# ScalarE in the order of the steps, e buffers in turn, and a shorter VectorE queue ahead of transposed steps

## The chip, the cores and the metric

The kernel runs on one core of a Trainium2 chip. Five engines work side by side, each through its own queue of instructions: TensorE (PE) multiplies matrices, VectorE (DVE) and ScalarE (ACT) work elementwise, GpSimd (POOL) gathers here, and SyncE (SP) starts DMAs. The metric is device time in microseconds (us), the median of several executions. A profile is one more execution, taken by the hardware profiler.

## The reference

The input is four images of 128 channels and 64 x 64 positions. Layer 0 normalizes in groups of channels, runs a deformable 3 x 3 convolution and adds its result to the image. A small convolution yields for every position and tap two offsets and a mask (a sigmoid); each tap then samples the image bilinearly at the offset place. Layer 1 treats the 4,096 positions as tokens of 128 channels: a layer norm; an attention of 16 heads of width 8, in which query, key and value are the same array (products of cosines), so that its score matrix is symmetric; layer norm; a feed-forward part of which only 8 channels' cosines enter; a second norm; and then a mixture of 8 experts, in which every token takes the weighted sum of its best two. In short, for each image:

```python
x = x + deformable_conv(group_norm(x))
t = tokens(x); u = layer_norm(t)
q = ring_of_cosines(u + rx)                      # 16 heads of 8
a = softmax(q @ q.T / sqrt(8)) @ q               # 4096 x 4096 per head
x1 = layer_norm(u + a @ w_comb.T + b_comb)
f  = relu((cos(x1[..., :8]) * cos(ry)) @ w1.T) @ w2.T
t  = t + layer_norm(x1 + f)
t  = t + top2_of_8_experts(layer_norm(t))
```

The largest part by far is the attention: 4 x 16 score matrices of 4096 x 4096 with one exponential for each element that is not had from symmetry.

## The kernel before

**Steps.** The attention is cut into runs. A run is a batch b, a group g of four heads and a chunk sc of 512 queries; it goes through key tiles t of 128 keys. A step is one (run, t): `scores` (line 1240) issues four matmuls on 32 rows each (line 1250) into two PSUM tiles `sc`, and two exps on ScalarE (line 1259), which write two tiles `e` of 128 x 1024. `context` (line 1263) multiplies each of the four heads' part of `e` with the values (line 1267) and adds into `acc`; at the end of a run VectorE copies `acc` out (line 1471 or 1473). There are 3,700 steps and 7,400 exps. The scores are issued `LAG` = 2 steps ahead of the context, so TensorE's order is: scores of step n + 2, some side matmuls, context of step n.

**Buffers.** `sc` comes from a pool of three PSUM buffers (line 254, two banks each), `e` from six buffers (line 1258, `bufs=6`). A buffer is free again once all that read it have done so.

**Weights from symmetry.** The exps of queries sc against keys sc + 1 are the transposes of those of queries sc + 1 against keys sc. For a step in the set `gives` the function `turn` (line 1131) has VectorE transpose the two `e` tiles in 32 x 32 blocks into a staging tile `st` (line 1141), which four DMAs store in `etd`; 396 of the 3,700 steps are such. A later run fetches them (line 1185) and multiplies them as side work in `from_turned` (line 1203). `st` has three buffers (NST), which the deformable convolution's `tr` tiles share.

**Side work.** All the rest runs beside the steps. `prepare` makes a batch's convolution and its queries, keys and values, for the batch after the one in attention; `finish` does the output projection, the feed-forward part and the experts of a chunk whose four groups are done. Both are generators. At each `yield need(...)` they ask for time on TensorE and VectorE, and the planner `Beside` decides when the next piece is emitted. It keeps a clock (`now`, 1.82 us a step) and a time up to which VectorE is booked (`dve`). A piece for VectorE is let in only if `dve - now` is at most the `backlog` that the main loop gives: 1.5 in the first runs (`streaming`), later 3.2, and 0.4 in the last three steps of a run. `beside.later(when, emit)` puts an emission off until the planner's clock reaches `when`; this is used for DMAs and for GpSimd. Up to two `finish` jobs are active at once (line 1117), and their tiles share a pool of eleven buffers (`f2`).

**Who orders the queues.** The main loop stands inside `tc.manual_schedule` (line 1395) for PE, DVE, SP and POOL: these run in the order in which the program emits them. ScalarE is not among them. Its order, and which of a pool's buffers an exp's tile gets, come from the framework's scheduler, which works with its own estimate of when instructions end.

**ScalarE's other instructions.** The mask's exp `mk` in `rows_and_weights` (line 559, eight times) and the router's exp `ex` in `experts` (line 1017, 32 times), and at the start some DMAs that load weights.

Of the kernel before, what the change touches and what calls it, by code (L numbers as in the profile page):

```python
# [9 lines left out]
F32 = mybir.dt.float32  # L10
I32 = mybir.dt.int32
F32R = mybir.dt.float32r
AF = mybir.ActivationFunctionType
ALU = mybir.AluOpType
AX = mybir.AxisListType
PE = mybir.EngineType.PE
DVE = mybir.EngineType.DVE
SP = mybir.EngineType.SP
POOL = mybir.EngineType.Pool
PSUM = bass.MemoryType.PSUM  # L20
DRAM = bass.MemoryType.DRAM

P = 128
# [176 lines left out]
def need(pe=0.0, dve=0.0, lat=0.0, hold=False, after=0.0):  # L200

    return pe, dve, lat, hold, after


def ve(n, ops=1):

    return ops * (0.17 + n / 960.0)
# [6 lines left out]
def tr(n):  # L216

    return 0.13 + 0.115 * n
# [3 lines left out]
def kernel(  # L222
# [22 lines left out]
    nc = tc.nc  # L245
# [5 lines left out]
    big = ctx.enter_context(tc.tile_pool(name="big", bufs=1))  # L251
    work = ctx.enter_context(tc.tile_pool(name="work", bufs=2))
    dram = ctx.enter_context(tc.tile_pool(name="table", bufs=1, space=DRAM))
    ps_s = ctx.enter_context(tc.tile_pool(name="ps_s", bufs=3, space=PSUM))
    ps_a = ctx.enter_context(tc.tile_pool(name="ps_a", bufs=1, space=PSUM))
    ps_m = ctx.enter_context(tc.tile_pool(name="ps_m", bufs=1, space=PSUM))

    beside = Beside()
# [2 lines left out]

    progress = {}
    featuring = []

    summed = []


    alone = []

    def misc(name):  # L270
        if alone:
            return ps_s.tile([P, 2, 512], F32, tag="sc", name=name)[:, 0, :]
        return ps_m.tile([P, 512], F32, tag="misc", name=name)

    def by_columns(dst, lhsT, rhs, start, stop):
# [139 lines left out]
    for i in range(NFX):  # L415
        t = big.tile([P, 4, QR], F32, name=f"fx{i}")
# [91 lines left out]
    def offsets(b, xn, idx, wt, rest):  # L508


        xn3 = xn.rearrange("p (h w) -> p h w", w=WW)
        HB = NBLK // 2

        def temp(name, n, half):
            return work.tile([P, HB, n], F32, tag="p2", name=f"{name}{b}_{half}", bufs=NP2)

        def products(half, got):

            for n, k in enumerate((4, 0, 1, 2, 3, 5, 6, 7, 8)):
                for top in range(0, 8, 4):
                    last = n == KK - 1 and top == 4
                    yield need(pe=MM256, dve=ve(512) if last else 0.0, lat=0.2 if last else FREE, hold=not last)
                    if n == 0 and top == 0:
                        po = misc(f"om_ps{b}_{half}")
                        p3 = po.rearrange("p (h w) -> p h w", w=WW)
                    dy, dx = k // 3 - 1, k % 3 - 1
                    for c in range(4):
                        r0 = 32 * half + 8 * c  # L530
                        ra, rb_ = max(r0 + top, -dy), min(r0 + top + 4, HH - dy)
                        ca, cb = max(0, -dx), min(WW, WW - dx)
                        nc.tensor.matmul(  # L533
                            p3[32 * c : 32 * (c + 1), ra - r0 : rb_ - r0, ca:cb],
                            lhsT=wom_sb[:, k, :],
                            rhs=xn3[:, ra + dy : rb_ + dy, ca + dx : cb + dx],
                            start=(n == 0 and top == 0), stop=last,
                        )
            oc = work.tile([P, 512], F32, tag="p2", name=f"oc{b}_{half}", bufs=NP2)
            nc.vector.tensor_scalar(oc, po, bom_sb, None, ALU.add)  # L540
            yield need(pe=tr(4), dve=ve(432), lat=0.2)
            om = temp("om", 27, half)
            got.append(om)
            pt = misc(f"oc_ps{b}_{half}")
            for i in range(4):
                nc.tensor.transpose(
                    pt[:, P * i : P * (i + 1)], oc[:, P * i : P * (i + 1)], ident
                )
            nc.vector.tensor_copy(
                om.rearrange("p (c i) k -> p i c k", i=4),  # L550
                pt.rearrange("p (i c k) -> p i c k", c=4, k=32)[:, :, :, :27],
            )

        def rows_and_weights(half, om):
            blk = slice(HB * half, HB * (half + 1))

            yield need(dve=ve(288, 2))
            mk = temp("mk", KK, half)
            nc.scalar.activation(mk, om[:, :, 18:27], AF.Exp, scale=-1.0)
            p = om[:, :, 0:18]  # L560
            nc.vector.tensor_tensor(p, p, grid_sb[:, blk, :], ALU.add)
            nc.vector.tensor_scalar(p, p, LO, HI, ALU.max, ALU.min)
            yield need(dve=ve(288, 3))
            fl, up, ix = temp("fl", 18, half), temp("up", 18, half), temp("ix", KK, half)
            nc.vector.tensor_scalar(fl, p, ROUND, None, ALU.add)
            nc.vector.tensor_scalar(fl, fl, ROUND, None, ALU.subtract)
            nc.vector.tensor_tensor(up, fl, p, ALU.is_gt)
            yield need(dve=ve(288, 2))
            nc.vector.tensor_tensor(fl, fl, up, ALU.subtract)
            nc.vector.tensor_tensor(p, p, fl, ALU.subtract)  # L570
            yield need(dve=ve(144, 3) + 0.6)

            def of_axis(t, a):
                return t.rearrange("p j (k a) -> p j k a", a=2)[:, :, :, a]

            nc.vector.tensor_scalar(mk, mk, 1.0, None, ALU.add)
            nc.vector.reciprocal(mk, mk)
            nc.vector.tensor_scalar(
                ix, of_axis(fl, 0), float(TW), 2.0 * TW + 2.0, ALU.mult, ALU.add
            )  # L580
            nc.vector.tensor_tensor(idx[:, blk, :], ix, of_axis(fl, 1), ALU.add)
            yield need(dve=ve(288))

            nc.vector.tensor_scalar(up, p, -1.0, 1.0, ALU.mult, ALU.add)
            for dy in range(2):
                yield need(dve=ve(144, 3), lat=0.2)
                nc.vector.tensor_tensor(ix, of_axis(p if dy else up, 0), mk, ALU.mult)
                for dx in range(2):
                    nc.vector.tensor_tensor(
                        wt[:, blk, :, 2 * dx + dy], ix, of_axis(p if dx else up, 1), ALU.mult  # L590
                    )

        got = []
        yield from products(0, got)
        yield from rows_and_weights(0, got[0])
        yield from products(1, got)
        rest.append(rows_and_weights(1, got[1]))
# [322 lines left out]
    def feed_forward(b, ch, x4, a4):  # L920
# [12 lines left out]
        nc.vector.tensor_copy(zx[:, :, 0, :].bitcast(F32R), zf)  # L933
        nc.vector.tensor_tensor(zx[:, :, 2, :].bitcast(F32R), zf, zx[:, :, 0, :], ALU.subtract)
        nc.vector.tensor_copy(zx[:, :, 1::2, :], zx[:, :, 0::2, :])
        yield need(pe=tr(4), dve=ve(512), lat=0.2)
        pz = misc(f"z_ps{b}_{ch}")
        for i in range(4):
# [15 lines left out]
        for i in range(4):  # L954
            for f in range(FFN // P):
# [7 lines left out]
                    f == 0, f == FFN // P - 1,  # L963
                )
        nc.vector.tensor_tensor(a4, a4, pf.rearrange("p (i c) -> p i c", c=C), ALU.add)  # L965
        m = work.tile([P, 4], F32, tag="ln_m", name=f"m2{b}_{ch}")
        rs = work.tile([P, 4], F32, tag="ln_r", name=f"r2{b}_{ch}")
        yield from layer_norm_stats(a4, m, rs, "ln")
# [8 lines left out]
    def experts(b, ch, x4):  # L977
# [18 lines left out]
        lg, ex, eq, gt = small("lg"), small("ex"), small("eq"), small("gt")  # L996
# [17 lines left out]
        )  # L1014
        nc.vector.tensor_reduce(mx, lg, AX.X, ALU.max)
        nc.vector.tensor_tensor(lg, lg, bcx(mx), ALU.subtract)
        nc.scalar.activation(ex, lg, AF.Exp)
        for rnd in range(2):
            yield need(dve=ve(32, 7), lat=0.2)
            nc.vector.tensor_reduce(mx, ex, AX.X, ALU.max)  # L1020
# [221 lines left out]
    def scores(run, t):  # L1242
        b, g = runs[run][:2]
        ps = [
            ps_s.tile([P, 2, 512], F32, tag="sc", name=f"sc{run}_{t}_{pr}") for pr in range(2)
        ]
        kT, qT = keys[b, g, t // 4][0], queries[run]
        for i in range(4):
            h = 32 * i
            nc.tensor.matmul(  # L1250
                ps[i // 2][:, i % 2, :],
                lhsT=kT[h : h + 32, P * (t % 4) : P * (t % 4 + 1)],
                rhs=qT[h : h + 32, :],
                start=True, stop=True,
            )
        es = []
        for pr in range(2):
            e = work.tile([P, 2, 512], F32, tag="e", name=f"e{run}_{t}_{pr}", bufs=6)
            nc.scalar.activation(e, ps[pr], AF.Exp, scale=1.0 / math.sqrt(HD))  # L1259
            es.append(e)  # L1260
        return es
# [130 lines left out]
    es = []  # L1392
    n = issued = begun = 0
    beside.rate = 1.0
    with tc.manual_schedule(engines={PE, DVE, SP, POOL}):
        alone.append(True)
        beside.add("prepare", prepare(0), 2)
        while (0, 0) not in prepared:
# [3 lines left out]
        while n < len(steps):  # L1402
# [21 lines left out]
            if streaming:  # L1424
                backlog = 1.5
            else:
                backlog = 0.4 if at >= len(ts) - 3 else 3.2
            if b + 1 < NB:

                share = (n - begun) / (of_batch[b] - 80 - begun)  # L1430
                beside.rank("prepare", 2 if progress.get(b + 1, 0.0) > share else 0.5)
# [121 lines left out]
```

## Time and profile before

| | |
|---|---|
| median of 3 runs | 7,730.28 us (7,711.24 to 7,750.06) |
| the profiled execution's own time | 7,756.43 us |
| its span, first to last instruction | 7,754.7 us |
| ScalarE busy | 6,874.7 us, of which exps (line 1259) 6,871.4 |
| VectorE busy | 4,481.5 us, of which transposes of e (line 1141) 937.6 |
| mean granted TensorE clock | 0.964 |
| exps start and end at | 179.3 us and 7,670.3 us |

The profile gives, for a group of instructions, how often it ran, how long it was busy, and the idle time of its engine just ahead of it with what ended that idle time. "ACT e L1259 <- PE acc L1267" is read as: ScalarE stood idle before an exp of line 1259, and a context matmul of line 1267 released it. A wait on several things is put down to the one that came last. The ends of matmuls are modelled, and PE busy counts overlapped matmuls, so a busy share of PE is not a share of its peak.

### The profile page before, as it was taken

Reading aid. Unit: us, or ns where it says so; the run is one execution under the profiler, and the core shown is the slowest. Engines: PE = TensorE matmul, PEld = TensorE weight load, DVE = VectorE, ACT = ScalarE, POOL = GpSimd, SP = SyncE. Lnnn points to the kernel's source line nnn. Section 1 sums busy time; section 2 is a strip of 40 time slices with the busy share of each in tenths; the row PEclk is TensorE's granted clock in tenths of the full one; section 3 lists DMA queues with packets and bytes.
Section 4 is the critical chain, followed back from the end, with each engine's and each line's share of the span. In section 5 each row is a group of like instructions: output and inputs, shape, how many; then the busy total and the mean of one; then the engine's idle time right before and its main releaser. Section 6 shows DMA issues by size and latency. Waiting matters only on the chain.

```text
span 7754.7 us, 181999 instructions
## 1 busy us (share of the span) xinstructions
PE 7193.2 (93%) x73736; PEld 2531.8 (33%) x73736; DVE 4481.5 (58%) x8976; ACT 6874.7 (89%) x7441; POOL 1650.3 (21%) x1326
## 2 busy tenths in 40 slices
PE   3679899899999999999999989999999999999997
PEld 2222233223333333333333323333333333333333
DVE  6766356667444767766544667765444545545444
ACT  0569899789999899989999978889999999999995
POOL 5544034343001332422000333431000000000000
PEclk6889999999999999999999999999999999999998
DMA  5767477879557878888666788988665587777762
GB/s 182 219 208 226 133 233 234 276 240 288 158 161 216 256 231 269 284 257 244 199 179 186 234 259 277 300 279 260 187 181 162 151 255 237 247 239 251 241 217 75
DMA packets 922614, 1730.69 MB, mean 223 GB/s; under 512 B 169074, under 2 KB 393356, under 8 KB 871084
## 3 DMA queue, kind: packets, MB, share of 16 engines
q1 hardware_dynamic: 821918, 1412.48, 59.8%
q0 software_dynamic: 92160, 302.06, 11.9%
q8 instruction: 578, 9.47, 0.5%
q10 hardware_dynamic: 7694, 4.52, 0.2%
q14 instruction: 264, 2.16, 0.1%
HBM read 1059.11 MB, written 659.57 MB: 222 GB/s over the span
## 4 chain that ended last, share of the span: by engine, by line
PE 82%; DMA 6%; DVE 4%; issue 3%; ACT 3%; SPq 2%; POOL 0%; another core or an unknown queue 0%; ACTq 0%; DVEq 0%; POOLq 0%
PE acc L1267 40%; PE sc L1250 24%; PE acc L1203 5%; PE conv_ps L278 4%; PE e_ps L278 3%; ACT e L1259 3%; PE f_ps L278 2%; DMA et<-etd 1%; PE om_ps L533 1%; DMA sT<-smd 1%; DMA etd<-st 1%; PE ao_ps L278 0%; DVE st L1141 0%; DMA smd<-tr 0%; DVE v L645 0%
## 5 line engine op out<-in xcount | busy, mean ns | idle before, releaser
L1259 ACT ACTIVATE e<-sc 128x1024 f32<-128x1024 f32 x7400 | 6871.4, 1066 | 743.0 <-PE sc L1250 467.0
L1267 PE MATMUL acc<-e,qf 128*32 128x512 f32 x29600 | 3978.3, 607 | 36.9 <-DVE cu L1473 22.3
L1250 PE MATMUL sc<-qT,kT 32*128 32x512 f32 x14800 | 2396.8, 500 | 261.2 <-ACT e L1259 153.6
L1250 PEld LDWEIGHTS sc<-qT,kT 32*128 32x128 f32 x14800 | 958.7, 183 | 3672.2 <-ACT e L1259 3053.7
L625 POOL DMA_INDIRECT v<-tab,idx x1152 | 1447.0, 1256 | 1758.6 <-DVE tr L686 1119.4
L1141 DVE STREAM_TRANSPOSE st<-e 128x1024 f32<-128x1024 f32 x792 | 937.6, 1222 | 800.5 <-ACT e L1259 565.0
L1267 PEld LDWEIGHTS acc<-e,qf 128*32 128x32 f32 x29600 | 801.9, 110 | 609.6 <-issue 344.8
L393 POOL TENSOR_TENSOR r<-ln_t,expo 128x4 f32<-128x4 f32 x96 | 112.3, 1170 | 3142.6 <-DVE ln_t L391 3106.0
L645 DVE TENSOR_TENSOR v<-v,wt 128x1536 f32<-128x1536 f32 x384 | 666.0, 1734 | 99.0 <-DMA v<-tab,idx 78.6
L1203 PE MATMUL acc<-et,qf 128*32 128x128 f32 x12672 | 524.6, 282 | 39.5 <-DMA et<-etd 31.6
L1065 DVE TENSOR_TENSOR eo<-e_ps,gt 128x512 f32<-128x512 f32 x256 | 175.2, 686 | 542.7 <-PE e_ps L278 532.0
L1203 PEld LDWEIGHTS acc<-et,qf 128*32 128x32 f32 x12672 | 303.5, 110 | 241.6 <-issue 191.6
L650 DVE TENSOR_TENSOR v<-v 128x768 f32<-128x768 f32 x384 | 367.2, 956 | 9.7
L278 PE MATMUL conv_ps<-sT,wconv_sb 128*32 128x256 f32 x4320 | 352.4, 400 | 12.6 <-DMA sT<-smd 8.1
L1471 DVE COPY cu<-acc 128x512 f32<-128x512 f32 x128 | 88.5, 691 | 405.6 <-PE acc L1267 341.6
L686 DVE STREAM_TRANSPOSE tr<-v 128x128 f32<-128x128 f32 x1080 | 249.5, 282 | 34.5 <-DMA etd<-st 24.9
L651 DVE TENSOR_TENSOR v<-v 128x384 f32<-128x384 f32 x384 | 215.7, 562 | 13.3
L393 POOL TENSOR_TENSOR rstd<-lt_t,expo 128x4 f32<-128x4 f32 x32 | 59.4, 1857 | 525.6 <-DVE lt_t L391 494.9
L278 PE MATMUL f_ps<-w_sb,h 128*32 128x128 f32 x4096 | 166.6, 282 | 1.1 <-issue 1.0
L950 DVE TENSOR_SCALAR h<-h_ps,b_sb 128x512 f32<-128x512 f32 x128 | 95.0, 744 | 102.4 <-PE h_ps L948 90.3
L823 POOL COPY fx<-rn 128x512 f32<-128x512 f32 x32 | 26.8, 836 | 540.3 <-DVE rn L822 361.8
L965 DVE TENSOR_TENSOR a<-a,f_ps 128x512 f32<-128x512 f32 x32 | 22.0, 687 | 201.8 <-PE f_ps L278 201.8
(224 smaller groups left out, 3146.9 us busy)
## 6 DMA issues: line engine op xcount, KB each, us to landing
etd<-st SPq DMA_DIRECT2D x1584, 256.0 KB
et<-etd SPq DMA_DIRECT2D x396, 1024.0 KB
kT<-kTd SPq DMA_DIRECT2D x400, 256.0 KB
smd<-tr SPq DMA_DIRECT2D x360, 192.0 KB
sT<-smd SPq DMA_DIRECT2D x360, 192.0 KB
qf<-fqd SPq DMA_DIRECT2D x400, 144.0 KB
qT<-qTd SPq DMA_DIRECT2D x166, 256.0 KB
atd<-cu SPq DMA_DIRECT2D x128, 256.0 KB
```

The lines of the kernel that those rows point to most:

```text
L278: nc.tensor.matmul(dst[c : c + 32], lhsT=lhsT[:, c : c + 32], rhs=rhs, start=start, stop=stop)
L625: nc.gpsimd.indirect_dma_start(out=v[:, k, :], out_offset=None, in_=tab, in_offset=bass.IndirectOffsetOnAxis(ap=idx[:, j, kk : kk + 1], ax ...
L645: nc.vector.tensor_tensor(v4, v4, w12[:, :, None].to_broadcast([P, 12, C]), ALU.mult)
L650: nc.vector.tensor_tensor(v[:, :, : 2 * C], v[:, :, : 2 * C], v[:, :, 2 * C :], ALU.add)
L651: nc.vector.tensor_tensor(v[:, :, :C], v[:, :, :C], v[:, :, C : 2 * C], ALU.add)
L686: nc.vector.transpose(out=tr9[:, k, :, j % 4, :], in_=v[:, k, :C].rearrange("p (c i) -> p c i", i=32),)
L1065: nc.vector.tensor_tensor(ws[hf], pe.rearrange("p (e c) -> p e c", c=C), gt[:, i, 4 * hf : 4 * (hf + 1), None].to_broadcast([P, 4, C]), AL ...
L1141: nc.vector.transpose(out=st[:, :, 2 * pr : 2 * pr + 2, :].rearrange("p o h (q j) -> p o (h q) j", j=32), in_=es[pr].rearrange("p h (q o i ...
L1203: nc.tensor.matmul(acc[32 * h : 32 * (h + 1), P * kt : P * (kt + 1)], lhsT=qf[:, t, QW * h : QW * h + 32], rhs=e[:, :, h, 32 * t : 32 * (t ...
L1250: nc.tensor.matmul(ps[i // 2][:, i % 2, :], lhsT=kT[h : h + 32, P * (t % 4) : P * (t % 4 + 1)], rhs=qT[h : h + 32, :], start=True, stop=True,)
L1259: nc.scalar.activation(e, ps[pr], AF.Exp, scale=1.0 / math.sqrt(HD))
L1267: nc.tensor.matmul(acc[32 * h : 32 * (h + 1), :], lhsT=qf[:, t % 4, QW * h : QW * h + 32], rhs=es[h // 2][:, h % 2, :], start=(t == ts[0]) ...
```

## The change

ScalarE joins the engines that run in program order, and the tiles that its exps read and write get their buffer by counting. `in_turn` gives the k-th tile of a kind the buffer k modulo n, by a tag of its own with one buffer: `sc` over three, `e` over six. Since program order now decides ScalarE's queue, the two small exps are no longer emitted on the spot but put off until the planner's clock reaches the time up to which VectorE is booked at that moment (`beside.later(beside.dve, ...)`); the piece after `mk`'s is put off by `lat=0.5`, so that `mk` is emitted before its reader.

In the main loop, outside the first runs and outside the last three steps of a run, the backlog is cut from 3.2 to at most 1.2 where one of the steps n to n + 3 is still in `gives`. A transposed step leaves `gives` when its transposes are emitted, one step ahead, so this concerns the two steps before that.

`feed_forward` gets a turn-taking: a job that reaches the point after `zx` waits, 0.5 at a time on the planner's clock, while another job is between there and the addition of `f_ps`.

```diff
-    ps_s = ctx.enter_context(tc.tile_pool(name="ps_s", bufs=3, space=PSUM))
+    ps_s = ctx.enter_context(tc.tile_pool(name="ps_s", bufs=1, space=PSUM))
...
+    feeding = []
...
+    taken = {}
+
+    def in_turn(pool, tag, n, shape, name, dt=F32):
+        k = taken[tag] = taken.get(tag, -1) + 1
+        return pool.tile(shape, dt, tag=f"{tag}{k % n}", name=name, bufs=1)
 
     def misc(name):
         if alone:
-            return ps_s.tile([P, 2, 512], F32, tag="sc", name=name)[:, 0, :]
+            return in_turn(ps_s, "sc", 3, [P, 2, 512], name)[:, 0, :]
...
-            yield need(dve=ve(288, 2))
+            yield need(dve=ve(288, 2), lat=0.5)
             mk = temp("mk", KK, half)
-            nc.scalar.activation(mk, om[:, :, 18:27], AF.Exp, scale=-1.0)
+            beside.later(
+                beside.dve,
+                lambda: nc.scalar.activation(mk, om[:, :, 18:27], AF.Exp, scale=-1.0),
+            )
...
         nc.vector.tensor_copy(zx[:, :, 1::2, :], zx[:, :, 0::2, :])
+
+        while feeding:
+            yield need(lat=0.5)
+        feeding.append(True)
         yield need(pe=tr(4), dve=ve(512), lat=0.2)
...
         nc.vector.tensor_tensor(a4, a4, pf.rearrange("p (i c) -> p i c", c=C), ALU.add)
+        feeding.clear()
...
-        nc.scalar.activation(ex, lg, AF.Exp)
+        beside.later(beside.dve, lambda: nc.scalar.activation(ex, lg, AF.Exp))
...
-            ps_s.tile([P, 2, 512], F32, tag="sc", name=f"sc{run}_{t}_{pr}") for pr in range(2)
+            in_turn(ps_s, "sc", 3, [P, 2, 512], f"sc{run}_{t}_{pr}") for pr in range(2)
...
-            e = work.tile([P, 2, 512], F32, tag="e", name=f"e{run}_{t}_{pr}", bufs=6)
+            e = in_turn(work, "e", 6, [P, 2, 512], f"e{run}_{t}_{pr}")
...
-    with tc.manual_schedule(engines={PE, DVE, SP, POOL}):
+    with tc.manual_schedule(engines={PE, DVE, SP, POOL, ACT}):
...
                 backlog = 0.4 if at >= len(ts) - 3 else 3.2
+
+                if any(step in gives for step in steps[n : n + 4]):
+                    backlog = min(backlog, 1.2)
```

More of the change, by code (lines that the diff above doesn't have):

```diff
@@ L19 @@
 POOL = mybir.EngineType.Pool
+ACT = mybir.EngineType.Activation
 PSUM = bass.MemoryType.PSUM
```

## The prediction

> **What bounds the kernel now.** I read the page first, its busy shares and the chain that ended last:
>
> ```profile
> PE 7193.2 (93%) x73736; PEld 2531.8 (33%) x73736; DVE 4481.5 (58%) x8976; ACT 6874.7 (89%) x7441; POOL 1650.3 (21%) x1326
> PE 82%; DMA 6%; DVE 4%; issue 3%; ACT 3%; SPq 2%; POOL 0%; another core or an unknown queue 0%; ACTq 0%; DVEq 0%; POOLq 0%
> ```
>
> TensorE (PE) and ScalarE (ACT) are both nearly full. A step is two exps and eight matmuls L1267. In quiet stretches exps start 0.904 us apart, so 1.81 us a step; the 3,700 steps then need 6,697 us, but the exps spread from 179 us to 7,670 us, 7,491. Some 794 us are lost, and the question is where. The windows view on L1259 (start:end, length, ACT busy, exps, granted clock, DMA share, GB/s):
>
> ```profile
> 180.00:1060.00 880.00, 683.39 (x735) 0.89 0.64 194
> 1060.00:1700.00 640.00, 556.71 (x598) 0.95 0.81 253
> 1700.00:2330.00 630.00, 596.34 (x645) 0.99 0.69 211
> 2330.00:3600.00 1270.00, 1135.48 (x1219) 0.98 0.82 255
> 3600.00:4100.00 500.00, 497.39 (x539) 1.00 0.65 190
> 4100.00:5250.00 1150.00, 1008.82 (x1083) 0.97 0.83 259
> 5250.00:7670.00 2420.00, 2392.36 (x2587) 1.00 0.69 213
> ```
>
> The stretch from 3,600 us runs at 500/269.5 = 1.855 us a step, that from 4,100 us at 1150/541.5 = 2.12. The slow stretches are those where the next batch is prepared beside the steps. The waits of ScalarE name two causes:
>
> ```profile
> ACT e L1259 <- PE sc L1250: 467.0, 205, 124.9
> ACT e L1259 <- PE acc L1267: 155.1, 140, 2.7
> ...
> ACT e L1259 <- PE acc L1203: 8.6, 6, 2.6
> ACT e L1259 <- DVE st L1141: 8.2, 4, 5.8
> ```
>
> The first is the start (124.9 us at once, before the first exp) and a TensorE that is late. The second is odd: an exp waits for a context matmul, which reads an e buffer. The timeline near 2,656 us shows one such spell:
>
> ```profile
> 2655.08 1.04 PE L1267 MATMUL acc<-e,qf 128*32 128x512 f32 x8
> ...
> 2656.21 1.94 ACT L1259 ACTIVATE e<-sc 128x1024 f32<-128x1024 f32 x2 [1.23 <-PE acc L1267]
> ...
> 2657.29 0.51 PE L1250 MATMUL sc<-qT,kT 32*128 32x512 f32 x2 [0.74 <-ACT e L1259]
> ...
> 2658.18 1.04 PE L1267 MATMUL acc<-e,qf 128*32 128x512 f32 x8
> ...
> 2659.32 1.94 ACT L1259 ACTIVATE e<-sc 128x1024 f32<-128x1024 f32 x2 [1.17 <-PE acc L1267]
> ```
>
> Context, exp, scores, context: each waits for the one before, and a step takes 2659.32 - 2656.21 = 3.11 us. There are six e buffers, three steps' worth, so an exp that takes the oldest should find it free. The allocation, which the profile doesn't show but the program of the kernel before does, explains it: all 7,400 exps stand in step order already, but only 6,974 take the buffer written six exps earlier; 267 take the one written four earlier, 29 five, 124 eight to sixteen. The allocator, left free on ScalarE, believed that VectorE would hold a buffer for its transposes, and gave the exp one whose context matmul comes later on TensorE. The detour lasts until a next transposed step mends it: 64 spells, 163 steps, 184 us over 1.81 a step, nearly all within the three slow stretches.
>
> **What the Trainium skill says.** "ScalarE: Activation LUTs", section "What ACT_TABLE_LOAD costs", prices an ACTIVATE at 186 + 0.833 N ns with 93 ns of overlap back to back: 946 ns for N = 1024, an estimate; the trace has 904 start to start, so the floor is the instruction itself. "PSUM — Partial Sum Buffer", section "Engine vs sequencer instructions", says that ScalarE's and VectorE's queues are strict FIFO: an exp that waits holds up all after it, as the spell shows. "TensorE: Matmul & The Clock Gate", section "What's actually happening", gives an idle TensorE half the clock, in windows of about 3.4 us; the trace agrees, with 1.00 granted in the smooth stretches and 0.95 to 0.98 in those with stalls.
>
> **The change part by part.**
>
> *Buffers in turn.* Every exp takes the buffer six back. Score tiles (sc) are three back already, so for them nothing moves. What goes is the waits on acc, 155.1 + 8.6 = 164 us. The count by steps gave 184; I keep the lower one, as steps with side matmuls cannot go below about 1.86 (in the chain 0.43 sc + 0.57 side + 0.86 acc).
>
> *Half clock.* 1 - clock, twice, is the time at half speed: 64 us, 51 and 69 in the three slow stretches, 184 in all. At half speed a step needs 3.7 us, so half of it, 92 us, is lost; 13 of the 31 windows there (the clock record of the trace) follow such a spell, 39 us. Between 0 and 39 comes back; I take 25.
>
> *The new wait.* An exp must now sit out late transposes of the step three back; behind it stand all later exps, and TensorE after them. From the trace, over 396 transposed steps: 23 end their transposes over 5.43 us (three steps) after their own exp began, by 83 us in sum; measured against when the exp three steps on really started, 11 steps and 37 us. Most is not queueing but VectorE itself waiting for a store to free its staging tile:
>
> ```profile
>   ACT e L1259: 565.0, 168
>   DMA etd<-st: 81.1, 19
>   DMA smd<-tr: 55.5, 11
> ```
>
> I take 60 us. The shorter side queue (1.2 us in place of 3.2 in the two steps ahead of a transposed one) mends only lateness with no idle gap before it, about 15 us of the 83. So 45 net; bounds 20 and 100.
>
> *mk and ex emitted later.* 8 and 32 instructions of 333 and 270 ns, as before. They now stand where the planner expects their input. Now they wait for almost nothing but once, where nothing follows (56.7 us in the last part):
>
> ```profile
>   DVE lg L1016: 57.1, 3
> ```
>
> If VectorE runs behind the planner, exps queue behind them: 40 times 0 to 1 us; I take 5, bound 40.
>
> *Side work held back.* The short limit and the turn-taking in feed_forward can only delay side work. Batch preparation has cover: the last keys (L839) of batches 1 to 3 come at steps 824, 1692 and 2501, needed at 964, 1876 and 2788, over 140 steps early. The close of a chunk is covered by the next chunk's steps except for the last: the output before the last is issued at 7,683 us, 13 us after the last exp, so a delay there adds to the end directly. 5 us, bounds 0 and 30; without cover a whole feed_forward would be about 25.
>
> *Less slack for transfers.* The slow stretches have DMA 81 to 83% busy and get some 5% shorter. What waits on DMA (v 79 us, et 32 + 36, sT 8, st and tr 160) grows; 20 us, bounds 0 and 60.
>
> Sum: -164 - 25 + 45 + 5 + 5 + 20 = -114. The profiled execution took 7,756.4 us (span 7,754.7), so 7,642; it was 26 us above the median of 7,730.3, which gives **7,616 us** for the median.
>
> **Rivals.**
>
> *The gain is larger*: VectorE has room (two thirds busy in the slow stretches), its lateness shrinks to about 20, TensorE keeps full clock, and transfers cost nothing: -164 - 39 + 20, some 7,545. For it: the stretch from 3,600 us, with transposed steps as dense, shows one such wait of 1.4 us and 1.855 a step. Against: DMA is at 65% there.
>
> *The wait moves to VectorE*: the late transposes are DMA-bound, and denser steps make them later: 100 us, plus 60 on transfers, no clock back, and the small items' 10: -164 + 170, about 7,735 at the bounds; with 80 and 45, 7,701. For it: 81.1 us on etd<-st. Against: 331 of the 337 lag-six reuses of a transposed buffer had it free in time.
>
> *Slower*: ScalarE blocked by ex and mk. Forty fixed places in a queue that was placed by a clock of 1.82 us a step; each us of average wait costs 40 us. It cancels the 114 at 2.9 us each and makes it 0.5% slower at (114 + 39)/40 = 3.8 us each; at 5 us, 7,816. For it: VectorE begins one in ten transposes over 2.2 us after its exp ended, one in a hundred over 9.4. Against: the median is 0.29.
>
> *The change does nothing*, since the order of exps is the same already: then 7,730. Against: the waits on acc exist and sit in the spells of early reuse.
>
> **How the numbers follow.** The main case has 0.52 and would lie within 7,560 to 7,680; the larger gain 0.16; the wait that moves 0.17; no effect 0.05; slower 0.10. About 0.5%, 39 us, is what a measurement here can tell from no change, so faster means below 7,691. The main case, the larger gain and a third of the moved wait count as faster: 0.74; the rest of the moved wait and no effect as the same: 0.16; slower 0.10. The range 7,530 to 7,735 leaves out the slower case and the far end of the larger gain, under 0.2.
>
> **What would show it.** In the profile after, ACT waits on acc L1267 near 10 us; ACT on DVE st up from 8 to 40 or 60; the stretch that took 2.12 a step under 2.0; clock above 0.964. If acc waits go and the time doesn't, look at DVE st and at DMA; if ex shows tens of us outside the end, ScalarE's queue was wrongly placed. Wrong I would be if the stalls labelled sc, 467 us with the start, follow from the same slowness of transfers and simply grow.

## The result, and the profile after

The changed kernel takes 7,695.06 us (median of 19 runs, 7,676.40 to 7,715.12), the kernel before 7,723.53 (19 runs, 7,711.24 to 7,750.06): a ratio of 0.9962, 95% interval 0.9953 to 0.9971. So 28 us were gained where 114 were forecast. The profiled execution of after has a span of 7,693.1 us, 61.6 less than that of before; the difference of the medians is smaller because before's profiled execution was itself 33 us above the median of its 19 runs, while after's is at its median.

| profiled execution | before | after |
|---|---|---|
| first to last exp | 7,491.0 us | 7,396.4 us |
| from the last exp to the end | 84.4 us | 115.1 us |
| ScalarE idle just ahead of exps | 743.0 us | 661.2 us |
| mean granted clock | 0.964 | 0.961 |

The page of after, its busy shares and the chain that ended last:

```profile
PE 7142.6 (93%) x73736; PEld 2515.1 (33%) x73736; DVE 4481.3 (58%) x8976; ACT 6861.6 (89%) x7441; POOL 1646.6 (21%) x1326
PE 80%; DMA 8%; DVE 5%; issue 3%; SPq 2%; ACT 1%; another core or an unknown queue 1%; POOL 0%; ACTq 0%; DVEq 0%; POOLq 0%
```

ScalarE went from 3% of the chain to 1%, DMA from 6% to 8%. The windows view on the exps, now L1277, with its columns as before (start:end, length, ACT busy, exps, clock, DMA share, GB/s):

```profile
2330.00:3600.00 1270.00, 1161.27 (x1252) 0.97 0.84 260
3600.00:4100.00 500.00, 494.68 (x536) 1.00 0.62 179
4100.00:5250.00 1150.00, 1044.25 (x1125) 0.98 0.84 260
```

The stretch from 4,100 us went from 2.12 us a step to 1150/562.5 = 2.04. The stretch from 3,600, where no batch is prepared, stays at 500/268 = 1.87. The gain is where it was sought, but the step stays above the 2.0 us that the prediction had named. What ScalarE waits for (total us, times, longest):

```profile
ACT e L1277 <- PE sc L1268: 511.1, 202, 124.0
ACT ex L1035 <- DVE lg L1034: 87.4, 2, 67.9
ACT e L1277 <- remote: 65.3, 26, 6.0
...
ACT e L1277 <- PE acc L1221: 20.6, 19, 3.4
ACT e L1277 <- DVE st L1159: 10.6, 5, 3.2
...
ACT e L1277 <- PE acc L1285: 3.3, 2, 1.8
```

The wait on a context matmul fell from 155.1 us to 3.3: all 7,394 exps after the first six now take the buffer six back, and the serial spells are gone. The new wait on transposes is 10.6 us. The waits on late scores grew from 467.0 to 511.1. The waits list over all engines says what TensorE, which is behind those scores, waits for, in before and then in after:

```profile
PE acc L1203 <- DMA et<-etd: 31.6, 13, 7.2
PE conv_ps L278 <- DMA sT<-smd: 8.1, 5, 3.1
```

```profile
PE acc L1221 <- DMA et<-etd: 50.8, 18, 8.6
...
PE conv_ps L288 <- DMA sT<-smd: 49.4, 10, 10.4
```

These are the fetched transposed tiles (`et`) and the samples for the convolution (`sT`). With the other lines of the list that end on a DMA, TensorE's matmuls wait 85 us for transfers in before and 149 in after. (The list has the waits on `et` a second time, under PEld, TensorE's weight loads: 36.2 and 56.5 us. These are the same waits and are not added.) Last, the end of the kernel, in the timelines: before has the output before the last 13 us after its last exp (7,670.3), after has it 44 us after its own (7,578.0).

```profile
7683.05 0.34 SPq L1081 DMA_DIRECT2D out_dram<-y_6T  x1
...
7726.97 0.23 ACT L1017 ACTIVATE ex<-lg 128x32 f32<-128x32 f32 x1 [56.68 <-DVE lg L1016]
```

```profile
7597.56 0.23 ACT L1035 ACTIVATE ex<-lg 128x32 f32<-128x32 f32 x1 [19.55 <-DVE lg L1034]
...
7621.74 0.34 SPq L1099 DMA_DIRECT2D out_dram<-y_6T  x1
...
7622.20 0.36 SPq L1117 DMA_DIRECT2D rdd<-rd  x1
```

In after (the second fence) the whole expert part of chunk 6 comes after the attention has ended, and only behind it does the last chunk's close go on (L1117). In the program, chunk 6's last feed-forward matmuls stand at step 3,665 of 3,700 in before and behind the last step in after.

Two suspects, then: the transfers in the steps, and the closing work in the tail. The experiments ran in sets, each with the kernel before in it and all on one chip, and the sets are of two kinds: before takes about 7,724 us in the first (A below, to which the result belongs too) and about 7,588 in the second (B). Every ratio is taken within one set. The expectations speak of two chips. The record gives each set a chip number, and the number 4 stands at a set of kind A (e9 to e12) and at one of kind B (e17, e18), so it is not shown that the kinds are chips.

### The profile page after: what moved, and what is told of

It reads as the page before. It is cut to its first block, busy times and chain, and to the rows that moved or that the text cites. A ratio compares the mean times of both kernels' runs of the same rounds, so it can differ in the third digit from the quotient of the medians.

```text
span 7693.1 us, 181975 instructions
## 1 busy us (share of the span) xinstructions
PE 7142.6 (93%) x73736; PEld 2515.1 (33%) x73736; DVE 4481.3 (58%) x8976; ACT 6861.6 (89%) x7441; POOL 1646.6 (21%) x1326
## 4 chain that ended last, share of the span: by engine, by line
PE 80%; DMA 8%; DVE 5%; issue 3%; SPq 2%; ACT 1%; another core or an unknown queue 1%; POOL 0%; ACTq 0%; DVEq 0%; POOLq 0%
PE acc L1285 39%; PE sc L1268 23%; PE acc L1221 5%; PE conv_ps L288 4%; PE e_ps L288 3%; DMA sT<-smd 2%; DMA et<-etd 2%; PE f_ps L288 2%; ACT e L1277 1%; PE om_ps L543 1%; DVE v L658 1%; DMA etd<-st 1%; DMA kT<-kTd 1%; DMA v<-tab,idx 0%
## 5 line engine op out<-in xcount | busy, mean ns | idle before, releaser
L1277 ACT ACTIVATE e<-sc 128x1024 f32<-128x1024 f32 x7400 | 6858.7, 1073 | 661.2 <-PE sc L1268 511.1
L1285 PE MATMUL acc<-e,qf 128*32 128x512 f32 x29600 | 3976.4, 606 | 40.3 <-DVE cu L1492 20.6
L1268 PE MATMUL sc<-qT,kT 32*128 32x512 f32 x14800 | 2342.8, 500 | 165.3 <-ACT e L1277 65.2
L1268 PEld LDWEIGHTS sc<-qT,kT 32*128 32x128 f32 x14800 | 942.2, 183 | 3538.8 <-ACT e L1277 3031.8
L1285 PEld LDWEIGHTS acc<-e,qf 128*32 128x32 f32 x29600 | 800.6, 110 | 613.3 <-issue 349.1
L1221 PE MATMUL acc<-et,qf 128*32 128x128 f32 x12672 | 523.8, 281 | 62.6 <-DMA et<-etd 50.8
L1221 PEld LDWEIGHTS acc<-et,qf 128*32 128x32 f32 x12672 | 303.0, 110 | 264.5 <-issue 195.8
L288 PEld LDWEIGHTS conv_ps<-sT,wconv_sb 128*32 128x32 f32 x4320 | 88.8, 109 | 193.8 <-issue 164.7
```

The costliest lines, as they stand in the source:

```text
L288: nc.tensor.matmul(dst[c : c + 32], lhsT=lhsT[:, c : c + 32], rhs=rhs, start=start, stop=stop)
L1221: nc.tensor.matmul(acc[32 * h : 32 * (h + 1), P * kt : P * (kt + 1)], lhsT=qf[:, t, QW * h : QW * h + 32], rhs=e[:, :, h, 32 * t : 32 * (t ...
L1268: nc.tensor.matmul(ps[i // 2][:, i % 2, :], lhsT=kT[h : h + 32, P * (t % 4) : P * (t % 4 + 1)], rhs=qT[h : h + 32, :], start=True, stop=True,)
L1285: nc.tensor.matmul(acc[32 * h : 32 * (h + 1), :], lhsT=qf[:, t % 4, QW * h : QW * h + 32], rhs=es[h // 2][:, h % 2, :], start=(t == ts[0]) ...
```

## The experiments

### Which part of the change does what

**e1: the change without the 1.2 limit.**

```diff
-                if any(step in gives for step in steps[n : n + 4]):
-                    backlog = min(backlog, 1.2)
```

> The changed kernel without the shorter limit on VectorE's queue (3.2 everywhere). My theory, that the limit delays the closing work of the chunks so that the last but one spills over the end: the time from the last exp to the end falls from 115 us to 85 to 95, ScalarE's waits on acc stay near 3 us, its waits on the transposes (DVE st) rise from 10.6 to 30 to 60, and the median is about that of the changed kernel or 20 us below, 7,675 to 7,700. Rival, that the limit is what keeps the buffers in turn from costing anything: DVE st over 80 us and a median at or above the kernel before, 7,720 or more.

Measured on A: 7,674.47 us, 0.9941 (0.9921 to 0.9962) of before's 7,723.72. The wait on acc L1285 is 1.0 us (once), that on transposes 27.5 us (7 times), and 80.0 us lie after the last exp. So the limit is a loss of some 20 us as a whole, though it does shorten the wait on transposes.

**e2: ScalarE in program order, but buffers from the pools.**

```diff
-            e = in_turn(work, "e", 6, [P, 2, 512], f"e{run}_{t}_{pr}")
+            e = work.tile([P, 2, 512], F32, tag="e", name=f"e{run}_{t}_{pr}", bufs=6)
```

(and the `sc` tiles from a pool of three in the same way)

> The changed kernel with ScalarE in program order, but sc and e from pools of three and six buffers as before. My theory, that the gain is the buffers and not the order: 138 exps of the 7,400 again take the buffer written four exps earlier, ScalarE waits 70 to 90 us on acc L1267's counterpart, and the median is 50 to 80 us above the changed kernel's, 7,745 to 7,775. Rival, that ScalarE's place among the engines in program order is what helps: acc waits near 3 us and a median of 7,685 to 7,705.

Measured on A: 7,752.18 us, 1.0037 (1.0022 to 1.0052). ScalarE's waits:

```profile
ACT e L1277 <- PE sc L1268: 505.6, 192, 121.9
ACT e L1277 <- PE acc L1285: 89.8, 77, 8.5
```

Program order alone does not end the early reuse: 138 exps still take the buffer four back, and the waits on acc are there. This kernel has the 1.2 limit too; e3 below has the limit without the order and comes to the same time (7,752.66 us). So the order brings nothing without the fixed buffers.

**e4: the kernel before with fixed e buffers only.**

```diff
-            e = work.tile([P, 2, 512], F32, tag="e", name=f"e{run}_{t}_{pr}", bufs=6)
+            e = in_turn(work, "e", 6, [P, 2, 512], f"e{run}_{t}_{pr}")
```

> The kernel before with only the e buffers in turn, ScalarE still ordered by the framework's scheduler. My theory, that both parts are needed: with fixed buffers the scheduler moves exps past each other instead of choosing another buffer (573 of the 7,400 no longer stand six places behind the last user of their buffer), so that a context matmul waits for an exp that was put behind its successors; stalls as many as before or more, median 7,720 to 7,800. Rival, that the fixed buffers alone do it: waits on acc under 30 us and a median of 7,640 to 7,690.

Measured on A: 7,801.41 us, 1.0095 (1.0077 to 1.0114).

```profile
ACT e L1264 <- PE sc L1255: 676.5, 372, 121.8
...
ACT e L1264 <- PE acc L1272: 4.5, 3, 2.3
```

The waits on acc are nearly gone, and those on scores are 209 us longer: the framework's scheduler, left free, now moved exps past each other (567 of 7,394 no longer take their buffer six exps later). Neither half helps alone; together they do.

**e3: the kernel before with the 1.2 limit only.** The two lines of e1, added to before.

> The kernel before with only the shorter limit on VectorE's queue. My theory: early reuse falls from 267 exps to 144, so waits on acc fall from 155 us to about 85, and the steps take some 60 us less; but the closing work of the last but one chunk starts six steps before the end, so the time after the last exp is 150 us or more in place of 84, and the median is 7,725 to 7,760. Rival, that the limit costs nothing: the time after the last exp stays near 84 us and the median is about 7,665.

Measured on A: 7,752.66 us, 1.0036 (1.0023 to 1.0049). Waits on acc fell to 93.4 us (85 times), since fewer exps got an early buffer, but 130.9 us lie after the last exp. The expected 150 or more was not reached; the direction and the place were right. In this execution the steps were 50 us shorter than in before's, whose profiled execution was 33 us above its median, and the tail 47 longer.

**e6: the kernel before with the turn-taking in `feed_forward` only.**

```diff
+        while feeding:
+            yield need(lat=0.5)
+        feeding.append(True)
         yield need(pe=tr(4), dve=ve(512), lat=0.2)
...
+        feeding.clear()
```

> The kernel before with only the turn-taking in feed_forward. My theory: it moves some closing work by a few steps and nothing else; waits on acc stay near 155 us, the time after the last exp near 85 us, and the median is within 10 us of the kernel before's, 7,714 to 7,734. Rival, that turn-taking is what lengthens the end: time after the last exp 100 us or more, median 7,740 or more.

Measured on B: 7,587.84 us, 1.0004 (0.9997 to 1.0011), with 84.1 us after the last exp. It costs and brings nothing there. The changed kernel without it was not run.

**e5: the kernel before, profiled again**, to see how much its first profiled execution was out.

> The kernel before once more, unchanged. Its profiled execution of 7,756 us was longer than each of its 19 timed ones. My theory, that some 33 us of the 92 us by which the steps shortened between the two profiles is that execution's own: here the last exp ends near 7,635 to 7,645 us and the time after it is again 84 us. Rival, that profile and timed runs differ by something outside the steps: the last exp again near 7,670 us.

It came to a set of kind B: 7,590.93 us. What was to be settled, where the 33 us of the first profiled execution lay, stays open. But its waits on acc, 159.0 us (143 times), are those of the first profile, so the term that the prediction took off was no accident of one execution.

### The tail

**e9 and e10: after, and after without the limit, once more.**

> The changed kernel once more, beside the others of this set on one chip. My theory, that chips differ by a fixed amount that the change doesn't touch: ratio to the kernel before 0.992 to 0.998 on this chip too, no waits on acc L1285 to speak of, the time after the last exp 115 us. Rival, that the small gain of the first measurement was that chip's: ratio 0.985 or less.

> The changed kernel without the shorter limit, again, so that the two versions with later requests can be set against it on one chip. My theory: ratio to the kernel before 0.992 to 0.996, and 15 to 30 us under the changed kernel. Rival, that the shorter limit pays where the chip has no other delays: at or above the changed kernel.

Measured on A, before at 7,725.20: 7,701.07 us, 0.9965 (0.9955 to 0.9976), and 7,684.33 us, 0.9948 (0.9929 to 0.9967). After the last exp lie 115.4 and 78.6 us. Between the two kernels lie 21 us (e1 against the result, two sets of kind A) and 17 us (here, within one set).

**e15: the limit lifted in the last batch only.**

```diff
-                if any(step in gives for step in steps[n : n + 4]):
+                if b + 1 < NB and any(step in gives for step in steps[n : n + 4]):
```

> The kernel after with the 1.2 limit lifted in the last batch only. Theory that the limit costs by the closing work that it pushes past the last exp: 78 to 90 us after the last exp where after has 115, and 15 to 35 us under after, so 7,665 to 7,685 where after takes 7,695 to 7,701. Rival, that the limit costs by its effect on the steps: within 10 us of after.

Measured on B: 7,515.30 us, 0.9898 (0.9883 to 0.9913) of 7,590.55. The output before the last is issued 9.6 us after the last exp again:

```profile
7419.17 6.59 ACT L1277 ACTIVATE e<-sc 128x1024 f32<-128x1024 f32 x7
...
7435.41 0.34 SPq L1099 DMA_DIRECT2D out_dram<-y_6T  x1
```

91.3 us lie after the last exp, one above the 78 to 90 expected and 24 less than in after. After itself did not run on B, so the gain over it in median time is not measured. But lifting the limit at the end alone is no worse than lifting it everywhere (0.9926 on B, e17 below), which points to the last batch as the place of what the limit costs. That it helps in the first three is hinted at and not settled: the two ratios are of different comparisons, and their intervals touch.

### The transfers

**e13 and e14: the fetches left out of both kernels.** `from_turned` multiplies two tiles that are filled once; the 396 loads of 1 MB go, all matmuls stay.

```diff
-        e = turned_tile(run, kt)
-        nc.sync.dma_start(
-            out=e.rearrange("p r h x -> p (r h x)"),
-            in_=etd[g][par][kt].rearrange("p r x -> p (r x)"),
-        )
+        if not kept_et:
+            for i in range(2):
+                e = turned_tile(i, i)
+                nc.vector.memset(e, 0.001)
+                kept_et.append(e)
+        e = kept_et[kt % 2]
```

> The kernel before, with the fetches of the transposed tiles left out: from_turned multiplies two tiles that are filled once with a constant, so that its matmuls stay and its 1-MB loads go. The output is not the reference's. Theory that transfers took the gain: before loses about the 35 us that TensorE waits on et, and some waits on st; 7,640 to 7,700 on a chip where before takes 7,725. Rival, that the loads are hidden: within 15 us of before. The question is answered by the next run against this one.

> The kernel after without the 1.2 limit, with the fetches left out in the same way (output not the reference's). With fetches it was 41 to 46 us below before. Theory that the fetches' lateness took the rest of the expected gain: now 80 to 120 us below the kernel before without fetches, waits of ScalarE on late scores clearly under the 343 us that they had. Rival, that the gain was never larger and the profiled execution of before overstated it: 30 to 60 us below it.

Measured on B, before at 7,590.55: before without fetches 7,525.33 us, 0.9920 (0.9906 to 0.9933); the changed kernel (no limit) without fetches 7,392.98 us, 0.9744 (0.9730 to 0.9757). With no fetches in either, the change without its limit brings 132 us, more than the 80 to 120 expected. ScalarE's waits, before without fetches and then the changed kernel without them:

```profile
ACT e L1262 <- PE sc L1253: 326.2, 66, 121.5
ACT e L1262 <- PE acc L1270: 191.9, 178, 2.7
...
ACT e L1262 <- DVE st L1141: 6.2, 2, 5.5
```

```profile
ACT e L1280 <- PE sc L1271: 364.3, 74, 120.5
...
ACT e L1280 <- DVE st L1159: 33.5, 8, 10.4
```

191.9 us go, 38.1 come back as late scores and 27.3 as late transposes: -126.5, close to the 132. This is about the balance that the prediction expected. But part of it is that before has more to lose here: its waits on acc are 191.9 us without the fetches and 159.0 with them (e5 below).

**e17 and e18: the changed kernel (no limit), with and without its fetches, on one chip.**

> The kernel after without the 1.2 limit and with its fetches, for the pair with the next run on one chip. On the chip where before takes 7,725 it gave 0.9941 and 0.9948. Where before takes 7,590 it is new: before without fetches was 65 us under before there, so if the fetches cost the changed kernel no more than that, it lies 65 us above 7,393, at 7,458, a ratio of 0.983. If its faster steps make the fetches cost twice as much: 7,520 or more, 0.991 to 0.994.

> The same with the fetches left out (output not the reference's). The distance to the run before this one is what the fetches cost the changed kernel: about 65 us if no more than in the kernel before, 110 to 150 us if they took the rest of the gain. Against before: 0.972 to 0.977 on either chip.

Measured on B, before at 7,588.33: 7,531.14 us, 0.9926 (0.9911 to 0.9940), and 7,391.28 us, 0.9741 (0.9726 to 0.9756). The fetches cost the changed kernel 140 us and the kernel before 65. So with the fetches the change brings 75 us less than the 132 that it brings without them. (The 57 that are left are e17's own distance to before, 7,588 less 7,531, and no second measurement.) The waits of TensorE on `et`, in the kernel before on B (e5) and then in the changed kernel (e17):

```profile
PE acc L1203 <- DMA et<-etd: 45.7, 14, 8.9
```

```profile
PE acc L1221 <- DMA et<-etd: 67.3, 14, 9.8
```

The same number of waits, each longer: 22 us more in sum. That is far from 75, so the direct wait is only a part. Nor did the fetches as a whole lose time to land: from the issue of a fetch to the moment at which TensorE reached its tile, the median over the 396 is 16.0 us in both traces. What grew is the number of tiles reached within 10 us of the issue, from 11 to 17; in both, the waits over 0.3 us come where less than 13 us are left. (These counts are made from the traces, fetch by fetch.) And the waits of ScalarE in e5 and then in e17:

```profile
ACT e L1259 <- PE sc L1250: 408.4, 90, 120.0
ACT e L1259 <- PE acc L1267: 159.0, 143, 2.7
```

```profile
ACT e L1277 <- PE sc L1268: 485.5, 98, 120.1
...
ACT e L1277 <- DVE st L1159: 34.2, 14, 8.2
```

From e5 to e17 the waits on acc go (159.0), 77.1 come back on scores and 14.8 on transposes: -67, where the two spans differ by 71. The waits on scores grow by 77.1 us with the loads, and by 38.1 (e14) and 48.0 (e18) without them. So of the 75 us some 33 are waits on acc that only the kernel without fetches had to lose, and 29 to 39 are late scores that come with the loads; the waits on transposes grow less with the loads than without, by 9 to 13. That makes 53 to 59; the rest is not found in these waits. TensorE's waits on all transfers tell the same: 109 us in e5 and 174 in e17, 59 in e13 and 92 in e14. Even without the loads they grow, mostly those on `sT`. The experiment takes away the waits and also 415 MB of traffic (HBM read 1,059 MB with, 644 without), so how much of the 75 is the wait of `from_turned` itself and how much the delay that these loads give to others is not separated. On A no kernel ran without its fetches.

**e7, e8, e16: the readers of a transfer put off.** The planner lets the matmuls of `from_turned` in once the fetch is 16 us old by its clock; e8 and e16 make that 20. In e7 the convolution's reads of `sT` are put off instead. All are without the 1.2 limit.

```diff
-        fetched[run, kt] = e, beside.now + 16.0
+        fetched[run, kt] = e, beside.now + 20.0
```

```diff
-            yield need(lat=6.0)
+            yield need(lat=9.0)
             get(1)
-            yield need(lat=4.0)
+            yield need(lat=9.0)
```

> The changed kernel without the shorter limit, and with the convolution asked for 8 us later on the planner's clock after its sT tiles are fetched (9 and 9 in place of 6 and 4). My theory, that a part of the gain is spent by TensorE waiting for sT: that wait falls from 31.5 us to under 8, and the median is 10 to 30 us below the one without the shorter limit, 7,645 to 7,665. Rival, that these waits lie beside others: the wait goes, the median stays at 7,670 to 7,680.

> The changed kernel without the shorter limit, and with the matmuls on fetched transposes asked for 20 us after the fetch on the planner's clock in place of 16. My theory, that another part is spent by TensorE waiting for et: that wait (47.5 us) falls to under 25, and the median is 10 to 30 us below the one without the shorter limit, 7,645 to 7,665. Rival, that two et buffers cannot give more time, so that the matmuls bunch at the end of a run: median 7,675 or more.

> The kernel without the 1.2 limit and with et asked for at 20 us in place of 16, which gave 0.9891 on a chip where before takes 7,585. If what the lateness costs is the same on every chip: 0.987 to 0.991. If it depends on the chip, as the run with both delays hints (0.9922 on the other chip): 0.992 to 0.995.

Measured on B. e7: 7,531.52 us, 0.9930 (0.9914 to 0.9947), no better than e17's 0.9926. Its waits on `sT` fell from 45.6 us to 13.2 and the time is the same. The waits of exps on transposes doubled instead, from 34.2 us in e17:

```profile
ACT e L1277 <- DVE st L1159: 73.3, 15, 10.3
```

So taking a wait from TensorE is not yet a gain. e8: 7,501.50 us, 0.9891 (0.9875 to 0.9908); e16, the same kernel: 7,495.42 us, 0.9884 (0.9868 to 0.9899). That is 83 and 95 us under before, and some 26 to 38 better than e17. TensorE waits 33.5 us (e8) and 41.3 (e16) for `et`, where it was 67.3. The kernel before was not run with 20 us, so how much of this gain belongs to the change is not shown.

**e11 and e12: both delays together, and a delay of 24 us.**

> Without the shorter limit, and with both requests later (sT 9 and 9, et 20). My theory, that the two waits add up: both waits of TensorE under half of those without it, the median 60 to 90 us below e10's kernel. Rival, that what one lets go the other takes (DMA queues full, transposes later): within 20 us of e8's ratio of 0.989.

> Without the shorter limit, and with the matmuls on fetched transposes asked for 24 us after the fetch: double the step from 16 to 20. My theory, that each us of lead takes a part of the waits for et: these under 15 us, the median 10 to 25 us below the one with 20 (ratio near 0.987). Rival, that four fetches through two buffers no longer fit into a run, so that TensorE is forced to wait at the run's end: ratio 0.990 or more.

Measured on A: 7,658.91 us, 0.9922 (0.9900 to 0.9943), and 7,715.95 us, 0.9991 (0.9984 to 0.9998). e11 is 25 us better than e10, less than the 60 to 90 expected, and their intervals overlap. In e12 no matmul waits for `et` any more, and most of the gain is lost:

```profile
ACT e L1277 <- PE sc L1268: 545.4, 280, 122.5
ACT e L1277 <- DVE st L1159: 59.9, 12, 11.0
```

What is not done by the last step of a run is emitted there all at once (`beside.drain("turned")`), and the next scores behind it are those of the following run's third step. Adding up by how much exps start over 0.905 us after the one ahead (only those over 0.3 us, from 1,000 us on), 166 of 450 us fall on third steps in e12, 11 of 392 in e10. The waits on scores are in sum what they were (540.8 in e10): what the loads no longer cost, the bunched work costs. The waits on transposes are 30 us longer (59.9 against 30.1), and that is most of the loss. Of the leads that were run the middle one is best: with 16 us TensorE waits for the load; with 24 the work is bunched at the end of the run.

## Why the prediction was wrong, step by step

**Buffers in turn, -164.** Right in mechanism and size. Waits on acc went from 163.7 us (both lines) to 23.9, of which 20.6 are behind L1221, the multiplication of fetched tiles; on B all 159.0 us went (e5, e17). e2 and e4 show that it takes both the order and the fixed buffers.

**Half clock, -25.** It did not come back: 0.964 to 0.961, and 0.972 to 0.969 without fetches (e13, e14). By the clock record, the time at half speed between 1,000 us and the last exp even rose, from 191 us to 212 (on B from 178 in e5 to 208 in e17). So the half-clock windows do not go when the spells go; what brings them on in after is not shown. By the prediction's own rule, half of that time is lost, so this term is some 10 to 15 us of loss and no gain.

**The new wait, +45.** Too high: 8.2 to 10.6 us with the limit, 8.2 to 27.5 and 30.1 without it (e1, e10). Where readers were put off it did reach 55 to 73 us (e8, e7). The limit does shorten this wait, by 17 to 23 us (10.6 and, in e9, 7.3 with it).

**mk and ex, +5.** Nothing in the steps: both waits on `ex` in after lie behind the last exp, and `mk` waits once, 6.6 us, at the start. The rival that made this the bound is out.

**Side work held back, +5, bounds 0 and 30. Wrong in size, at the upper bound.** The place was named, "the output before the last is issued at 7,683 us, 13 us after the last exp, so a delay there adds to the end directly", and then priced near nothing. The limit pushed this work out of the last steps: 84.4 to 115.1 us after the last exp in the profiles, 17 to 21 us between the medians with and without the limit. The "whole feed_forward" that the prediction put at "about 25" without cover was nearer.

**Less slack for transfers, +20, bounds 0 and 60. This is the step that failed.** The mechanism was named and priced at a third of its size or less. TensorE's waits on transfers grew from 85 us to 149 on A and from 109 to 174 on B (e5, e17), by 64 and 65; and taking the fetches out of both kernels raises what the change brings from 57 us to 132 (B, without the limit), by 75. The prediction counted what waited on DMA in the trace of before, its `et` twice (32 + 36 is one wait, seen by the matmuls and by the weight loads), and let it grow by a fixed 20. It did not ask what these waits become where steps no longer stall. That the stalls of the old spells had given the fetches time to land fits the longer waits, but the traces show it only for some: the median lead of a fetch is the same 16.0 us, and 17 tiles in place of 11 are reached within 10 us. How the rest arises is open.

**The sum.** In the prediction's terms the two profiles of A show: some 140 us of waits on acc gained where 164 were forecast; late scores 44 us longer, where the late transfers show; the 25 of the clock not got; transposes 2 in place of 45; the tail 31 in place of 5. In medians: 57 us on B (e17) and 41 to 49 on A (e10, e1) without the limit, 24 to 28 on A with it. These are the measured distances themselves and not a check of the terms.

**The profiled execution.** The sum used its 7,756.4 us and took 26 off, as stated; that does not bear on the gain. But a comparison of the two profiles would have shown 62 us where the medians show 28.

**The rivals.** "The wait moves to VectorE" gave 7,701 to 7,735, nearest to the 7,695 measured, but that is luck: the wait did not move to VectorE (10.6 us) but to TensorE, and from there to late scores. "The gain is larger" (183 us) comes nearest when the fetches are out (132). The last sentence of the prediction, that it would be wrong if the stalls labelled sc "simply grow", is the one that came true in its number, 467.0 to 511.1, and in part in its cause. The measured time is 0.4% under before, inside the band called the same, which had been given 0.16.

**Still open.** How the 75 us divide into the wait for `et` and the load on the DMA queues; whether the limit helps in the first three batches; whether 20 us for `et`, best on B, is best on A, where only 16, 20 with `sT` moved, and 24 were run; what the kernel before would gain from 20 us; and why A and B differ.

## What to carry to other kernels

When a serial stall is taken out, look for transfers in the same stretch: here TensorE's waits on them grew from 109 us to 174, which the trace of the slower kernel did not tell. Price it by taking the transfer out of both kernels, and look at what else that changes in each. Then set its lead time anew (here that made 83 to 95 us out of 57; with too long a lead nearly all was lost). Work that closes a kernel has no cover behind the last step, so a limit that holds back side work should be lifted there.

## What was not expected of the hardware

The same kernel takes 7,684 us in one set (e10) and 7,531 in another (e17), and before 7,724 and 7,588. Both of these sets have the chip number 4, so the record does not say whether the chip or something else differs. ScalarE's idle time ahead of exps explains nearly all of it. In the page's groups (calls, busy and mean ns, then idle time ahead), the changed kernel without the limit on A (e10):

```profile
L1277 ACT ACTIVATE e<-sc 128x1024 f32<-128x1024 f32 x7400 | 6865.3, 1075 | 674.3 <-PE sc L1268 540.8
```

on B (e17):

```profile
L1277 ACT ACTIVATE e<-sc 128x1024 f32<-128x1024 f32 x7400 | 6852.3, 1071 | 529.5 <-PE sc L1268 485.5
```

and a wait of ScalarE in e10 that e17 has not at all ("remote": what ended it is not in the profile):

```profile
ACT e L1277 <- remote: 56.4, 24, 6.0
```

The exps take the same time (1,075 and 1,071 ns); on A they are released late more often: 305 exps start over 0.3 us late, 132 on B. From 700 us on, e10 has 134 exps ahead of which ScalarE sits idle for over 0.3 us although in the last 0.3 us before their start neither their own scores, nor the exp before, nor the context matmuls of three steps back, nor any transpose has ended by the trace; they start 1.6 us after the modelled end of their scores (median), and their idle time sums to 166 us. In e17 there is none. The Trainium skill, "Perfetto Trace Analysis", section "Summary: the profiler window per engine type", says that a TensorE record's end is estimated and that the passing on of the semaphore is not in it; so such a delay may lie where the trace has no record, and no run here shows its cause.
